# Turning all rows of the attention matrix on VectorE, and the identity in the diagonal tiles of adj, in a two-layer graph kernel

## The chip, the cores and the metric

The kernel runs on one core of one Trainium2 chip. The metric is the device time of one execution in microseconds. The kernel before was timed in three runs: median 2083.7 us, from 2083.01 to 2084.57. One more execution was profiled.

## What is computed

There are 3327 nodes with 256 features each and a weighted adjacency matrix adj. The first layer mixes over two graphs, in two steps, and the second is a graph attention layer with four heads. Cut to what matters:

```python
# layer 0, on h = relu(layernorm(x)); R = (adj + I) with rows scaled to sum 1
for n in range(2):
    logits = (Xa @ W1.T @ W2.T) @ (Xa @ W3.T).T
    probs = softmax(logits)
    A = probs kept down to the smallest set with sum >= 0.9, rows scaled to sum 1
    Xf = R @ Xf
    Xa = A @ Xa
    Z = Z + Xf @ U1[n].T + Xa @ U2[n].T
x = x + layernorm(h + Z) * ln_g + ln_b
# layer 1, on h = relu(layernorm(x)); hp = h @ W in 4 heads of 64; s, d from hp and a
e = leaky_relu(s[:, None] + d[None, :], 0.2), -inf where adj <= 0
x = x + elu(softmax(e) @ hp)
```

## The kernel before

The nodes are padded to 26 tiles of 128 (NT = 26, NP = 3328). Everything is f32. The fast path (function fast) is one list of pieces of work; a second, general path runs only if a check on the numbers at the end asks for it, and it doesn't here.

**Order.** Class Plan (L472) holds the pieces. put (L481) adds one with its engine, a planned length, a rank, the pieces it needs, the buffers it takes and gives, and a delay until others see its result (LAG). order (L507) plays this through in planned time, on each engine always taking the ready piece of lowest rank, and issue (L581) writes the instructions in the order found. The order on each engine's queue is therefore fixed when the program is built, and rests on the planned lengths. Pieces that issue nothing (a function `lambda: None`) join several needs or give back a buffer; they sit on SyncE's or GpSimd's list with lengths of 0.0 or 0.02. either (L500) leaves a piece to whichever of two engines is free.

**Stages.** First, x is loaded, normalised and projected (prepare, project_u). Then come two steps over the 26 rows of tiles (a row is 128 nodes against all 3328). Last, layer 1 runs in four blocks of 832 target nodes (attend_neighbours, L1629).

**A row of a step** (class Row, L873; search and attention, L1506 and L1563):
- TensorE makes the logits (L907) and ScalarE their exponentials in e, with sums (exps, L916). The pieces are 1024, 1024, 1024 and 255 wide.
- ScalarE counts entries above a guess, in passes over the whole row (L961, about 3 us each), GpSimd steps the guess on single columns, and VectorE collects the largest candidates (window, sort) and finds the threshold (choose, L1046). drop (L1074) sets what is under it to zero, in four pieces.
- e has then to be turned, since it stands with its targets on the partitions and TensorE needs its sources there. For rows under BLOCKED (all 26 of step one, 23 of step two), the first 24 tiles go through VectorE, in pairs of tiles interleaved element by element: turn_blocks (L1112) turns 32x32 blocks in place, put_blocks writes 1024 columns to blocks in DRAM, and get_blocks reads them back in four transfers, each onto 32 partitions. The last two tiles, and all 26 tiles of the other three rows, are turned by TensorE into a px bank (turn, L1084) and copied to et by ScalarE or VectorE (turned, L1097).
- attend_blocks (L1125) and attend (L1102) multiply with rhs into the bank acca.

**A full row** (class Full, L1139; full, L1604) is adj's row times Xf. adj comes in from HBM in seven loads of four tiles (load, L1146, four at buffers), and 26 products go to the bank accf (some, L1151). adj lacks the identity, so in step one add (L1181) adds the row's own tile and 1.0 to the sum, and in step two own (L1355) adds the row's own tile to ys before ys is stored.

**Layer 1.** Per block and source tile, ScalarE makes a mask from adj (L1753, L1754), VectorE writes masked exponentials for four heads in one e buffer (L1765), and TensorE multiplies: product (L1774) into the banks pl, sums (L1789) into acca and accf, sums after every second tile. After 26 tiles leave (L1839) copies the banks out, and seven pieces of 128 nodes are turned (L1868), divided, put through elu, added and stored.

Buffers on chip: e has four, used by rows and then by layer 1 (mine, L1814), which adds three more (e2) in the memory of c and rhs once the rows are done; px has two banks, et three buffers, at four.

Of the kernel before, what the change touches and what calls it, by code (L numbers as in the profile page):

```python
# [25 lines left out]
H = 4  # L26
# [23 lines left out]
BLOCKED = (NT, NT - 3)  # L50
# [421 lines left out]
class Plan:  # L472
# [3 lines left out]
    LAG = {"PE": 0.2, "ACT": 0.2, "DVE": 0.15, "POOL": 0.1, "SP": 2.2}  # L476
# [23 lines left out]
    def either(self, first, second, rank, *args, **kw):  # L500

        p = self.put(*first[:2], rank, first[2], *args, **kw)
        p["on"] = {e: (length, fn, self.LAG[e], 0.0) for e, length, fn in (first, second)}
        p["engine"] = ""
        return p
# [82 lines left out]
def fast(  # L588
# [58 lines left out]
    with ExitStack() as l0:  # L647
# [24 lines left out]
        blocks = spill.tile([3, 4, P, 2 * P], F32, name="blocks")  # L672
# [28 lines left out]
        def weights():  # L701
# [39 lines left out]
            a = plan.put("PE", 0.25, -200.0, turn, take=["px"], needs=[plan.put("SP", 0.02, -201.0, lambda: None, lag=8.0)])  # L741
# [126 lines left out]
        plan = Plan(dict(rows=1, mvs=3, pl=2, px=2, acca=1, accf=1, et=3, at=4, y=1, e2=3, mask=2, e5=1, qg=2, **BUFS))  # L868
# [4 lines left out]
        class Row:  # L873
# [3 lines left out]
                "b w t0 t1 t2 u g k2 p0 p1 p2 p3 D0 D1 D2 v z r0 s0 s1 s2 h x th tq mid dh kh fl d up h0 h1 room zs cnt "  # L877
# [38 lines left out]
            def exps(self, k):  # L916
                pl = self.pl.pop(k)
                to = self.e[:, PART * k : PART * k + pl.shape[1]]
                if k < 3 and self.i < BLOCKED[self.n]:
                    to = to.rearrange("p (g q t) -> p g t q", g=4, t=2)  # L920
                    pl = pl.rearrange("p (g t q) -> p g t q", g=4, t=2)
                S.activation(  # L922
                    to,
                    pl,
                    AF.Exp,
                    accum_out=(self.p0, self.p1, self.p2, self.p3)[k],
                )

            def row_sum(self):
                k = self.NAMES.index("p0")  # L930
                S.activation(self.sc[:, k + 4 : k + 8], self.sc[:, k : k + 4], AF.Copy, accum_out=self.s)
# [114 lines left out]
            def choose(self):  # L1046
# [14 lines left out]
                V.scalar_tensor_tensor(out_, win, nxt, keep, ALU.is_gt, ALU.mult, accum_out=self.cnt)  # L1061
                V.tensor_sub(self.m, met[:, 2, i], self.cnt)
                ties = small.tile([P, PIECES * 8], F32, name="rest", bufs=1).rearrange("p (c r) -> p c r", r=8)
                V.tensor_scalar(ties, self.cands, nxt, None, ALU.is_equal)
                num, upto = (small.tile([P, 4], F32, name=name, bufs=1) for name in ("num", "upto"))
                V.tensor_reduce(num[:, :3], ties[:, :15, :].rearrange("p (a c) r -> p a (c r)", a=3), AX.X, ALU.add)
                V.tensor_reduce(num[:, 3:], ties[:, 15, :], AX.X, ALU.add)
                V.tensor_tensor_scan(upto, num, num, 0.0, ALU.add, ALU.bypass)
                V.scalar_tensor_tensor(num, upto, self.m, num, ALU.is_le, ALU.mult, accum_out=met[:, 4, i])
                self.thr = small.tile([P, 4], F32, name="thr")  # L1070
                V.tensor_scalar(upto, upto, self.m, 2.0**-24, ALU.is_gt, ALU.mult)
                V.tensor_scalar(self.thr, upto, 1.0 - 2.0**-24, nxt, ALU.add, ALU.mult)

            def drop(self, o):  # L1074

                piece = self.e[:, o * PART : min((o + 1) * PART, N)]
                V.scalar_tensor_tensor(piece, piece, self.thr[:, o : o + 1], piece, ALU.is_gt, ALU.mult)  # L1077
# [6 lines left out]
            def turn(self, g):  # L1084
                m = min(4, NT - 4 * g)
# [1034 lines left out]
```

## Time and profile before

| | us |
|---|---|
| median of three runs | 2083.7 |
| the profiled execution, whole | 2085.48 |
| its span, first to last instruction | 2083.6 |
| TensorE busy in it | 2036.4 |
| VectorE busy | 1730.6 |
| ScalarE busy | 1298.7 |
| GpSimd busy | 999.0 |
| mean granted TensorE clock | 0.994 of full |

By time, the load and projection take about the first 90 us, the two steps run to about 1600 us, and layer 1 runs from about 1605 to the end. A line of a group in the prediction reads: line of the kernel, engine, operation, what is written and read with its shape, number, then busy time and mean ns of one, then the engine's idle time just before the group and what ended it. In a line of waits, the time in total is followed by the number of waits and the longest. In a line of stretches come the stretch and its length; busy time and number of instructions for TensorE's matmuls, its weight loads, VectorE, ScalarE and GpSimd; the granted clock; the DMA engines' busy share; and GB/s. An f32 matmul shows as two instructions, a transpose as one.

### The profile page before, as it was taken

Reading aid. Unit: us, or ns where it says so; the run is one execution under the profiler, and the core shown is the slowest. Engines: PE = TensorE matmul, PEld = TensorE weight load, DVE = VectorE, ACT = ScalarE, POOL = GpSimd, SP = SyncE. Lnnn points to the kernel's source line nnn. Section 1 sums busy time; section 2 is a strip of 40 time slices with the busy share of each in tenths; the row PEclk is TensorE's granted clock in tenths of the full one; section 3 lists DMA queues with packets and bytes.
Section 4 is the critical chain, followed back from the end, with each engine's and each line's share of the span. In section 5 each row is a group of like instructions: output and inputs, shape, how many; then the busy total and the mean of one; then the engine's idle time right before and its main releaser. Section 6 shows DMA issues by size and latency. Waiting matters only on the chain. (4 is left out here: it accounts for less than half of the span.)

```text
span 2083.6 us, 34334 instructions
## 1 busy us (share of the span) xinstructions
PE 2036.4 (98%) x10695; PEld 1417.9 (68%) x10695; DVE 1730.6 (83%) x4105; ACT 1298.7 (62%) x2480; POOL 999.0 (48%) x2170
## 2 busy tenths in 40 slices
PE   8999999999999999989999999999999999999997
PEld 6477778877787878767778787788877333333332
DVE  5689897778876871578998989988987999999895
ACT  5776665666556611777778776778662547474552
POOL 5476665456544620567878778787872000000001
PEclk9999999999999999999999999999999999999999
DMA  4166676557666674786666767677633444444341
GB/s 116 42 191 187 192 192 192 167 154 200 192 183 180 181 200 128 203 218 176 178 189 176 210 179 193 190 202 193 184 114 113 144 140 140 132 139 117 113 126 34
DMA packets 580513, 338.56 MB, mean 162 GB/s; under 512 B 327931, under 2 KB 533281, under 8 KB 580321
## 3 DMA queue, kind: packets, MB, share of 16 engines
q1 hardware_dynamic: 579424, 336.06, 57.3%
q8 instruction: 87, 1.43, 0.3%
q14 instruction: 106, 0.86, 0.2%
q10 hardware_dynamic: 896, 0.21, 0.0%
HBM read 242.86 MB, written 93.05 MB: 161 GB/s over the span
## 5 line engine op out<-in xcount | busy, mean ns | idle before, releaser
L961 ACT ACTIVATE junk<-e,sc 128x3327 fp8e5<-128x3327 f32 x147 | 450.9, 3067 | 26.2 <-POOL sc L998 24.7
L1130 PE MATMUL acca<-rhs,e 128*128 128x256 f32 x1872 | 426.9, 381 | 0.6 <-DMA e<-blocks 0.3
L1130 PEld LDWEIGHTS acca<-rhs,e 128*128 128x128 f32 x1872 | 365.7, 197 | 43.0 <-issue 3.5
L1155 PE MATMUL accf<-c,at 128*128 128x256 f32 x1352 | 315.0, 384 | 13.7 <-ACT main L1166 5.4
L1155 PE MATMUL accf<-main,at 128*128 128x257 f32 x1352 | 315.8, 383 | 3.0 <-ACT main L1306 2.5
L1155 PEld LDWEIGHTS accf<-c,at 128*128 128x128 f32 x1352 | 252.5, 191 | 63.0 <-ACT main L1166 8.4
L1155 PEld LDWEIGHTS accf<-main,at 128*128 128x128 f32 x1352 | 252.4, 191 | 51.9 <-issue 11.2
L1024 DVE MAX8 cands<-y 128x8 f32<-128x205 f32 (+1 forms) x832 | 243.1, 362 | 3.6
L1920 POOL TENSOR_TENSOR qq<-qq 128x256 f32<-128x256 f32 x4 | 3.0, 756 | 457.0 <-ACT qq L1916 457.0
L1019 DVE SCALAR_TENSOR_TENSOR y<-e,sc 128x1639 f32<-128x1639 f32 x84 | 165.1, 1965 | 57.4 <-POOL sc L1009 56.2
L922 ACT ACTIVATE e<-pl 128x1024 f32<-128x1024 f32 (+1 forms) x168 | 152.7, 919 | 77.6 <-PE pl L907 67.9
L1754 ACT ACTIVATE et<-at 128x448 bf16<-128x448 f32 (+1 forms) x204 | 112.5, 551 | 130.0 <-DVE e L1765 74.2
L1781 PE MATMUL pl<-e,main 128*64 128x416 f32 x1024 | 190.4, 517 | 0.1
L1077 DVE SCALAR_TENSOR_TENSOR e<-e,thr 128x1024 f32<-128x1024 f32 (+1 forms) x168 | 177.6, 1061 | 2.6 <-DMA qg<-kqs 0.2
L907 PE MATMUL pl<-kt,qg 64*128 64x512 f32 (+1 forms) x832 | 173.8, 536 | 0.3 <-ACT qq L922 0.3
L1114 DVE STREAM_TRANSPOSE e<-e 128x1024 f32<-128x1024 f32 x117 | 146.0, 1248 | 3.7
L1781 PEld LDWEIGHTS pl<-e,main 128*64 128x64 f32 x1024 | 70.3, 137 | 111.1 <-issue 92.3
L1765 DVE SCALAR_TENSOR_TENSOR e<-c,low,et 128x832 f32<-128x832 f32 x128 | 128.9, 1076 | 6.0 <-issue 3.2
L907 PEld LDWEIGHTS pl<-kt,qg 64*128 64x128 f32 x832 | 71.5, 186 | 83.2 <-issue 76.8
L1753 ACT ACTIVATE at<-at 128x448 f32<-128x448 f32 (+1 forms) x204 | 110.8, 543 | 24.7 <-DMA at<-in_adjt_dram 24.5
L1765 DVE SCALAR_TENSOR_TENSOR e<-qq,low,et 128x832 f32<-128x832 f32 x120 | 120.6, 1081 | 4.1 <-PE accf L1795 2.9
L961 ACT ACTIVATE junk<-qq,sc 128x3327 fp8e5<-128x3327 f32 x35 | 107.3, 3066 | 8.5 <-POOL sc L998 8.2
(550 smaller groups left out, 3550.5 us busy)
## 6 DMA issues: line engine op xcount, KB each, us to landing
at<-in_adjt_dram SPq DMA_DIRECT2D x414, 256.0 KB
blocks<-e SPq DMA_DIRECT2D x117, 512.0 KB
e<-blocks SPq DMA_DIRECT2D x468, 128.0 KB
at<-in_adjt_dram SPq DMA_DIRECT2D x102, 192.0 KB
blocks<-qq SPq DMA_DIRECT2D x30, 512.0 KB
qq<-blocks SPq DMA_DIRECT2D x120, 128.0 KB
at<-in_adjt_dram SPq DMA_DIRECT2D x52, 128.0 KB
ys<-ystage SPq DMA_DIRECT2D x26, 256.0 KB
```

What stands on the lines that cost most here:

```text
L907: T.matmul(pl[:, lo : lo + m], qg[self.n, self.i // 4][half, self.i % 4, :], kt[half, 512 * k : 512 * k + m], start=True, stop=True,)
L922: S.activation(to, pl, AF.Exp, accum_out=(self.p0, self.p1, self.p2, self.p3)[k],)
L961: S.activation(junk[:, :N], self.e[:, :N], fn, bias=t, scale=-1.0, accum_out=dst, saturate=False)
L1019: V.scalar_tensor_tensor(self.y[:, : hi - lo], self.e[:, lo:hi], self.up, self.e[:, lo:hi], ALU.is_lt, ALU.mult, accum_out=(self.h0, self. ...
L1024: V.max(self.cands[:, a * PIECES // 2 + k, :], self.y[:, at[k] - lo : at[k + 1] - lo])
L1077: V.scalar_tensor_tensor(piece, piece, self.thr[:, o : o + 1], piece, ALU.is_gt, ALU.mult)
L1114: V.transpose(part, part)
L1130: T.matmul(self.acc, lhs, rhs[self.n][:, j, :], start=(j == 0), stop=stop and j == js[-1])
L1155: T.matmul(self.acc[:, : self.w], self.at[j // JC][:, j % JC, :], self.src[:, j, : self.w], start=(j == 0), stop=(j == NT - 1),)
L1754: S.activation(to, src, AF.Sign)
L1765: V.scalar_tensor_tensor(held["e"][:, k, :], extra["both"][b % 2][:, k, :], low[:, j, k : k + 1], held["mask"], ALU.max, ALU.mult,)
L1781: T.matmul(q["acc"][a][k * FH : (k + 1) * FH, c, :C], main[:, j, h * FH : (h + 1) * FH], held["e"][:, h, c * C : (c + 1) * C], start=(j == 0),
```

## The change

All rows are turned through VectorE and DRAM, and turn, turned and attend are gone. A row now has three parts of 1024, 1024 and 1280 columns, for dropping, turning and the round trip. The last piece of exponentials is written in two halves to the interleaved places, so there are five partial sums for four. choose finds the threshold of each piece by a running count over all 128 candidates, in fewer instructions, and failures checks accordingly.

GpSimd adds the identity to the diagonal tile of each row of adj after it is loaded (diagonal). The additions of the own tile are gone from take, add and finish1. In finish2, ScalarE scales by qd straight from the bank, in four parts, and VectorE's scale is gone.

In the plan, pieces that issue nothing have their own list "" with length 0, many lengths and delays are set anew, and full rows of step one get later ranks. In layer 1 one of the extra buffers (ec, in the memory of c) may be used before all rows are done, the first two source tiles are ranked before the last rows of step two, and the sums of block 0 wait for all rows. In the last block the last six tiles (LATE) are done for the first 416 nodes and then for the other 416, and each half is copied out by itself.

The diff, cut to its core:

```diff
-    LAG = {"PE": 0.2, "ACT": 0.2, "DVE": 0.15, "POOL": 0.1, "SP": 2.2}
+    LAG = {"PE": 0.2, "ACT": 0.2, "DVE": 0.15, "POOL": 0.1, "SP": 2.2, "": 0.0}
...
-        plan = Plan(dict(rows=1, mvs=3, pl=2, px=2, acca=1, accf=1, et=3, at=4, y=1, e2=3, mask=2, e5=1, qg=2, **BUFS))
+        plan = Plan(dict(rows=1, mvs=3, pl=2, px=2, acca=1, accf=1, et=3, at=4, y=1, e2=2, ec=1, mask=2, e5=1, qg=2, **BUFS))
...
+                if k < 3:
+                    S.activation(to, pl.rearrange("p (g t q) -> p g t q", g=4, t=2), AF.Exp, accum_out=sums[k])
+                else:
+                    S.activation(to[:, 0, 0, :], pl[:, :P], AF.Exp, accum_out=self.p3)
+                    S.activation(to[:, 0, 1, : m - P], pl[:, P:], AF.Exp, accum_out=self.p4)
...
-                V.scalar_tensor_tensor(out_, win, nxt, keep, ALU.is_gt, ALU.mult, accum_out=self.cnt)
-                V.tensor_sub(self.m, met[:, 2, i], self.cnt)
-                ties = small.tile([P, PIECES * 8], F32, name="rest", bufs=1).rearrange("p (c r) -> p c r", r=8)
-                V.tensor_scalar(ties, self.cands, nxt, None, ALU.is_equal)
-                num, upto = (small.tile([P, 4], F32, name=name, bufs=1) for name in ("num", "upto"))
-                V.tensor_reduce(num[:, :3], ties[:, :15, :].rearrange("p (a c) r -> p a (c r)", a=3), AX.X, ALU.add)
-                V.tensor_reduce(num[:, 3:], ties[:, 15, :], AX.X, ALU.add)
-                V.tensor_tensor_scan(upto, num, num, 0.0, ALU.add, ALU.bypass)
-                V.scalar_tensor_tensor(num, upto, self.m, num, ALU.is_le, ALU.mult, accum_out=met[:, 4, i])
-                self.thr = small.tile([P, 4], F32, name="thr")
-                V.tensor_scalar(upto, upto, self.m, 2.0**-24, ALU.is_gt, ALU.mult)
-                V.tensor_scalar(self.thr, upto, 1.0 - 2.0**-24, nxt, ALU.add, ALU.mult)
+                V.scalar_tensor_tensor(out_, win, nxt, keep, ALU.is_equal, ALU.mult, accum_out=self.m)
+                ties = small.tile([P, PIECES * 8], F32, name="rest", bufs=1)
+                V.tensor_scalar(ties, self.cands.rearrange("p c r -> p (c r)"), nxt, None, ALU.is_equal)
+                V.tensor_tensor_scan(ties, ties, ties, 0.0, ALU.add, ALU.bypass)
+                self.thr = small.tile([P, PIECES], F32, name="thr")
+                V.tensor_scalar(self.thr, ties[:, 7::8], self.m, 2.0**-24, ALU.is_gt, ALU.mult)
+                V.tensor_scalar(self.thr, self.thr, 1.0 - 2.0**-24, nxt, ALU.add, ALU.mult)
+                ends = ties[:, 39:80:40]
+                V.scalar_tensor_tensor(ends, ends, self.m, ends, ALU.is_equal, ALU.mult, accum_out=met[:, 4, i])
...
+            def diagonal(self):
+                own = self.at[self.t // JC][:, self.t % JC, :]
+                GP.tensor_add(own, own, ident)
...
             def take(self):
                 self.f = small.tile([P, H * FH + 2 * H], F32, name="f", bufs=BUFS["f"])
-                V.tensor_add(self.f[:, :D], self.acc[:, :D], self.src[:, self.t, :D])
-                V.tensor_copy(self.f[:, D : D + 1], self.acc[:, D:])
-                self.added = True
+                V.tensor_copy(self.f[:, : self.w], self.acc[:, : self.w])
...
-            a = plan.put("DVE", 0.43, r + 0.3, own, needs=[a, fulls[t]], hold=0.4)
-            y = plan.put("SP", 0.5, r + 0.3, store, needs=[a], give=["ystage"], lag=3.0)
+            y = plan.put("SP", 0.5, r + 0.3, store, needs=[a], give=["ystage"], lag=7.0)
...
-                f = held["f"] = small.tile([P, H * FH + 2 * H], F32, name="f", bufs=BUFS["f"])
-                S.copy(f, held["pm"])
-                S.activation(qd[:, t, :], f[:, H * FH + H :], AF.Exp)
-                S.activation(low[:, t, :], f[:, H * FH + H :], AF.Exp, scale=ALPHA - 1.0)
+                pm = held["pm"]
+                S.activation(qd[:, t, :], pm[:, H * FH + H :], AF.Exp)
+                for k in range(H):
+                    part = slice(k * FH, (k + 1) * FH)
+                    S.activation(main[:, t, part], pm[:, part], AF.Copy, scale=qd[:, t, k : k + 1])
+                S.activation(low[:, t, :], pm[:, H * FH + H :], AF.Exp, scale=ALPHA - 1.0)
+                S.copy(sd[:, :, t, :], pm[:, H * FH :].rearrange("p (k h) -> p k h", k=2))
...
+            come = []
+            for g in range(3):
+                b = plan.put(
+                    "DVE", 1.17 if g < 2 else 1.44, rank - 1.001, row.turn_blocks, g, needs=[drops[g]]
                 )
+                b = plan.put("SP", 0.5, rank - 1.0, row.put_blocks, g, needs=[b], lag=8.0)
+                b = plan.put("", 0.0, -90.0, lambda: None, needs=[b], lag=0.0)
+                come.append(
+                    [plan.put("SP", 0.6, rank - 1.0, row.get_blocks, g, o, needs=[b], lag=5.5) for o in range(4)]
+                )
+            for j in range(0, NT - 2, 4):
+                js = range(j, j + 4 if j < 20 else NT)
                 a = plan.put(
+                    "PE", 0.432 * len(js), rank, row.attend_blocks, js, needs=[come[j // 8], a, right],
+                    take=["acca"] * (j == 0), give=[own_e[row.n][row.i]] * (j == 20),
                 )
...
+            a, own = None, plan.put("POOL", 0.4, -90.0, f.diagonal, needs=[loads[t // JC]])
             for j in range(0, NT, 2):
                 last = j % JC == JC - 2 or j == NT - 2
                 a = plan.put(
-                    "PE", 0.437 * 2, rank, f.some, range(j, j + 2), needs=[a, loads[j // JC], right[j : j + 2]],
+                    "PE", 0.437 * 2, rank, f.some, range(j, j + 2), needs=[a, loads[j // JC], right[j : j + 2], own if t in (j, j + 1) else None],
                     take=["accf"] * (j == 0), give=["at"] * last,
                 )
...
+                    if b == 3 and j >= NT - LATE:
+                        for c in range(2):
+                            r = rank if c == 0 else r0 + 9.0
+                            p_ = plan.put("PE", 0.71, r, product, 0, (c,), needs=[x_, last_acc, halves[c]])
+                            p_ = plan.put("PE", 0.71, r, product, 1, (c,), needs=[x_, y_, p_])
+                            halves[c] = plan.put(
+                                "PE", 0.76, r, sums, (c,), needs=[p_, last_den], give=[mine] if c else []
+                            )
+                        continue
...
-                full(n, t, (min(1.0 + 1.15 * t, 27.0) if n == 0 else base + 1.0 + t), [p[0] for p in sources], [p[1] for p in sources] if n == 0 else loaded[0])
+                full(n, t, (2.0 + 1.3 * t if n == 0 else base + 1.0 + t), [p[0] for p in sources], [p[1] for p in sources] if n == 0 else loaded[0])
```

## The prediction, made before the changed kernel ran

> **What bounds the kernel now.** I read the page's first part, then TensorE's groups with their shapes apart, then what TensorE waited for, then stretches of the span, then the timeline around the longest waits and the end.
>
> ```profile
> span 2083.6 us, 34334 instructions
> PE 2036.4 (98%) x10695; PEld 1417.9 (68%) x10695; DVE 1730.6 (83%) x4105; ACT 1298.7 (62%) x2480; POOL 999.0 (48%) x2170
> ```
>
> TensorE is busy 98% of the span, but its matmul ends are modelled, so I checked it by the distance from one start to the next in the trace's records. It is 216 ns (median; least 215) for each half of an f32 matmul of 256 columns, whether its left side came through TensorE (L1107) or through blocks (L1130), and 109 ns for a transpose; a record lasts 381 and 273 ns because neighbours overlap. TensorE therefore runs back to back, and the time is its work plus its gaps. The groups that the change touches, and a neighbour:
>
> ```profile
> L1130 PE MATMUL acca<-rhs,e 128*128 128x256 f32 x1872 | 426.9, 381 | 0.6 <-DMA e<-blocks 0.3 <-issue 0.2
> L1107 PE MATMUL acca<-rhs,et 128*128 128x256 f32 x352 | 86.2, 380 | 0.3 <-ACT xa L1134 0.3
> L1089 PE MATMUL px<-ident,e 128*128 128x128 f32 x156 | 27.5, 285 | 5.2 <-ACT ystage L1349 5.0 <-DVE e L1077 0.3
> L1089 PE MATMUL px<-ident,qq 128*128 128x128 f32 x20 | 4.0, 280 | 0.2 <-DVE qq L1077 0.2
> ```
>
> The 156 + 20 at L1089 are the transposes of e. The gaps, by TensorE's waits:
>
> ```profile
> PE accf L1155 <- ACT main L1166: 5.4, 5, 3.4
> PE px L1089 <- ACT ystage L1349: 5.0, 1, 5.0
> PE accf L1155 <- DMA at<-in_adjt_dram: 5.0, 1, 5.0
> PE accf L1155 <- DVE main L1169: 3.3, 3, 1.4
> ...
> PE accf L1155 <- ACT main L1306: 2.5, 1, 2.5
> ```
>
> All gaps over 0.1 us sum to 36.9 us: 7 to 8 in the first 45 us, 1.2 at the end, about 28 from 90 to 1550 us. Four of these are long (2.5 at 92 us, 5.0 at 736, 5.0 at 892, 3.35 at 1545, sum 15.8), and the clock answers them. The stretches around them, against undisturbed ones:
>
> ```profile
> 736.00:747.10 11.10, 6.13 (x17) 4.74 (x16) 7.43 (x21) 3.65 (x3) 5.83 (x10) 0.69 0.41 135
> 891.90:900.70 8.80, 3.83 (x11) 3.00 (x11) 8.59 (x21) 5.85 (x6) 7.03 (x15) 0.81 1.00 237
> 1544.50:1552.70 8.20, 4.85 (x19) 3.63 (x18) 7.69 (x27) 4.15 (x6) 5.83 (x12) 0.79 0.77 262
> 98.60:736.00 637.40, 636.95 (x2958) 505.32 (x2956) 536.96 (x1451) 414.24 (x750) 370.02 (x799) 1.00 0.67 186
> 1604.60:2068.90 464.30, 464.20 (x3393) 169.49 (x3392) 429.73 (x488) 251.19 (x597) 5.54 (x6) 1.00 0.43 125
> ```
>
> The clock is 0.69 to 0.81 in the first three and 1.00 in the others. The trace's clock records put it at one half for 17 us in all after the four waits (3.4, 6.8, 3.4, 3.4), some 8 us of work lost. Waits and slow clock make these four places worth about 24 us.
>
> [...]
>
> **The change part by part, against the profiled span of 2083.6.**
> 1. *Transposes leave TensorE.* 49 rows x 2 and 3 rows x 26 = 176, x 109 ns = 19.2 us. All lie on the engine that is never free, so all of it comes off. The matmuls behind them keep their number and 216 ns. **-19.2.**
> 2. *VectorE.* Transposes: 147 x 1.248 = 183 now, 52 x (2 + 1.25) x 1.248 = 211 after, +28. Drops: per row 3 x 1.265 + 0.45 = 4.24 becomes 3.25 x 1.265 = 4.11, -7. choose: the instructions from L1061 to L1072 take 1.93 us from start to start; in their place come a product with sum (0.33), a scan of 128, two small scalings (0.24 each) and one with sum (0.32). The scan is not in the trace: 24 elements take 207 ns and 32 take 273, by which 128 would take from 0.3 (4 elements: 178, so nearly flat) to 1.07 (that slope); I take 0.4, so 1.53 and -21 over 52 rows (+15 to -26). Copies of transposes (12.6), the self term at L1185, L1174 and L1186 (12.0), L1357 (12.6) and the scaling at L1457 and L1458 (15.7) go. Sum about -52 of 1731. VectorE is not what TensorE waits for (its releases in the list come to 5 us), so directly 0; it is slack against new waits.
> 3. *ScalarE, GpSimd, DMA.* ScalarE loses 18.9 us of copies at L1100 and gains about 0.3 x 52 for the split exponentials and 0.6 x 26 for scaling, +12 of 1299. GpSimd gains 52 additions of the identity; between 287 ns (128x1) and 826 ns (128x256) I take 0.55, 29 us on an engine that is busy 48%. DMA: the round trip goes from 49 x 12 to 52 x 13 tiles, 150 to 173 MB or 8% of the traffic in those stages, whose DMA share is 0.66. All beside TensorE: 0. If GpSimd's cover is gone, see rival 4.
> 4. *Waits that change.* The 5.0 us at 736 is a transpose of e that wants a px bank; the bank is held because ScalarE's copy to ystage waits for the store of ys (33 us of such waits at L1349). The transpose is gone, and the store no longer waits for the self term; that wait goes. The other three are results that stand behind a 3.06 us count on ScalarE (L1306, L1166) or a load that came late: matters of order. The order is planned anew: durations in it now meet the trace (transposes 1.17 for 1.25 planned, copies of exponentials 1.07), the store's delay is 7 for 3, and empty steps no longer take turns on SyncE and GpSimd. Bounds: all four places go (-24) or as many new ones come (+20 and more); I take half, **-12**.
> 5. *End of step two.* The last three rows now take the round trip. From the end of VectorE's transpose to the first matmul that uses it is 13.7 us at best and 18 in the median now, where TensorE's own path began within 2 us of the drops. The last row would be ready some 10 us later. Cover: products of stage three that need no sums. The five e buffers (four e, one ec) allow 5 x 2.8 = 14 us, with the first two tiles' masks ranked early. Bounds 0 and +12; **+3.**
> 6. *Last block of stage three.* The period of two tiles is 8.67 us, of which 8.38 is 64 half matmuls and 0.29 two changes of shape. Six tiles in 12 halves have 24 changes for 6, 18 x 0.145 = +2.6. After the last sum 4 of 7 pieces remain; these are spaced 0.75 us, so 3 x 0.75 = -2.3. Bounds -4 and +3; **0.**
>
> Sum -19.2 - 12 + 3 = -28, span 2055.4. The profiled run took 2085.5, the median is 2083.7; taking the difference from the median gives **2055**.
>
> **Rivals.**
> 1. *Most gaps go.* For it: one wait's cause is removed, and the plan's figures are nearer the trace. Against: a fixed order on six queues always misses somewhere. 2083.7 - 19.2 - 24 - 4 = 2036.
> 2. *The gain is half given back.* New waits of about 20 us take the place of the old (late blocks, a bank, ScalarE's counts). [...] 2083.7 - 19.2 + 10 = 2074.
> 3. *TensorE's transposes were free.* If they sat in gaps, nothing but the waits moves: about 2083. Against: 109 ns from start to start, with neighbours following directly.
> 4. *Slower: the identity.* Each full product now waits at tile t for a GpSimd addition. GpSimd works in order and stands up to 6.5 us before counts (91.5 us in 28 waits at L991). Pairing the loads of at with the first matmul that reads each, in order, 63 of 364 are used less than 6 us after issue, the median 13.0. If the addition came 1 us late in each of 52 products, +52 - 28: 2108. It decides from 28/52 = 0.54 us on average. Against: the order takes it ahead of other GpSimd work, and most loads have 8 us to spare.
>
> **How the numbers follow.** Forecast 0.54 (own range 2044 to 2067), rival 1 0.19, rival 2 0.15, rival 3 0.03, rival 4 0.09. Up to 2079 and down to 2034 leaves out rivals 3 and 4 and the lower part of rival 1, 2 in 10. What a measurement can tell is 0.2%, or 4 us. Faster than 2079.5: 0.86; slower than 2087.9: 0.10; between: 0.04.
>
> **What would show it.** Step 1: no transposes of e, 10519 TensorE instructions, still 216 ns apart. Step 2: VectorE near 1680 us busy. Step 4: fewer than four stretches of half clock, and no wait of px for ystage. Step 5: gaps around 1550 to 1610 us, released by blocks or e. Step 6: under 15 us from the last sum to the end. Rival 4: waits of accf for GpSimd on at. It is wrong if TensorE's gaps sum to over 65 us, whatever releases them, or if a 256-column half matmul is spaced otherwise than 216 ns.

## The result and the profile after

| | before | changed | ratio, 95% interval |
|---|---|---|---|
| median, first comparison | 2084.1 us (4 runs) | 2071.4 us (4 runs, 2066.6 to 2077.0) | 0.9944 [0.992, 0.9969] |
| the changed kernel again, another chip (e1) | 2081.7 us | 2072.5 us (6 runs) | 0.9952 [0.9938, 0.9967] |

The forecast was 2055. The change gains 9 to 13 us where 28 were forecast. The direction held, and so did the outer range of 2034 to 2079; the forecast's own range of 2044 to 2067 did not, nor did the size. The first part of the page, after:

```profile
span 2075.2 us, 33982 instructions
...
PE 2025.6 (98%) x10519; PEld 1401.3 (68%) x10519; DVE 1696.3 (82%) x3768; ACT 1298.7 (63%) x2630; POOL 1040.1 (50%) x2222
```

TensorE has the 10519 instructions that were forecast, 176 fewer, and is busy for the same 98% of a span that is only 8.4 us shorter. Its groups with shapes apart:

```profile
L1100 PE MATMUL acca<-rhs,e 128*128 128x256 f32 x2184 | 485.6, 380 | 4.1 <-DMA e<-blocks 2.3 <-DVE y L1016 1.1 <-ACT main L1139 0.6
L1125 PE MATMUL accf<-main,at 128*128 128x257 f32 x1352 | 323.8, 389 | 14.1 <-DMA at<-in_adjt_dram 7.6 <-POOL at L1132 3.3 <-ACT f L1136 1.7
L1125 PE MATMUL accf<-c,at 128*128 128x256 f32 x1352 | 308.6, 382 | 5.9 <-DMA at<-in_adjt_dram 2.2 <-POOL at L1132 2.2 <-ACT main L1139 1.1
```

The groups of transposes are gone, a record of L1100 (attend_blocks) lasts 380 ns, and starts still lie 216 ns apart. So the saved work is what was forecast. What moved stands behind the bars. L1125 is the product of a full row, L1155 in the kernel before; the lines with main are step one's, those with c step two's:

```profile
L1155 PE MATMUL accf<-main,at 128*128 128x257 f32 x1352 | 315.8, 383 | 3.0 <-ACT main L1306 2.5 <-ACT f L1162 0.5
L1155 PE MATMUL accf<-c,at 128*128 128x256 f32 x1352 | 315.0, 384 | 13.7 <-ACT main L1166 5.4 <-DMA at<-in_adjt_dram 5.0 <-DVE main L1169 3.3
```

Step one's products stand idle for 14.1 us where it was 3.0, mostly for loads of adj and for the identity, and step two's for 5.9 where it was 13.7. TensorE's waits of the changed kernel, longest first (us in total, times, longest):

```profile
PE accf L1125 <- DMA at<-in_adjt_dram: 9.8, 7, 4.2
PE accf L1125 <- POOL at L1132: 5.5, 3, 2.7
PE acca L1732 <- ACT xa L1104: 4.5, 1, 4.5
PE pl L906 <- ACT e L921: 2.4, 2, 1.3
PE acca L1100 <- DMA e<-blocks: 2.3, 2, 1.4
```

The 5.0 us for ystage and the waits for counts (main) that headed the list before are gone or small. In their place stand loads of adj, the identity's addition (L1132) and one copy of the last row's result (L1104). All gaps over 0.1 us sum to 40.2 us, for 36.9 before. The stretches around the longest, and an undisturbed one (columns as in the prediction):

```profile
753.00:758.00 5.00, 4.89 (x15) 4.09 (x16) 0.00 (x0) 0.00 (x0) 0.00 (x0) 0.66 1.01 246
783.00:793.50 10.50, 7.96 (x23) 5.22 (x24) 1.92 (x6) 1.84 (x4) 0.89 (x1) 0.67 0.63 210
1519.00:1525.00 6.00, 4.41 (x13) 3.33 (x14) 5.89 (x11) 0.60 (x1) 5.41 (x9) 0.72 1.07 252
1592.00:1604.00 12.00, 7.46 (x48) 2.68 (x48) 6.69 (x9) 5.81 (x12) 2.23 (x2) 0.86 0.68 217
98.60:736.00 637.40, 632.65 (x2900) 499.80 (x2899) 546.22 (x1375) 420.15 (x783) 409.48 (x845) 1.00 0.72 198
```

The clock is 0.66 to 0.86 in the first four. Stretches of half clock ahead of the tail sum to 23.9 us in six places, for 17.1 in four. In the first and third the DMA engines' busy share is 1.01 and 1.07.

**Stalls, the measure used below.** For each TensorE instruction I took the distance from its start to the next one's, less the undisturbed distance of that shape (216 ns for 256 columns, 109 ns for a transpose, 443 ns at a change of the tile's shape). The sum holds gaps and lost clock together. It is 71.9 us before and 82.5 after. So the span's -8.4 is -19.0 of work and +10.6 of stalls. Work here is counted, not measured: it is what the instructions would take at the undisturbed distances. Stalls by stretch of each kernel's own span, with those of the experiments:

| profiled execution | 0-110 | 110-680 | 680-960 | 960-1480 | 1480-1620 | to the end | sum |
|---|---|---|---|---|---|---|---|
| before | 15.9 | 4.3 | 21.3 | 13.9 | 8.9 | 7.5 | 71.9 |
| before, figure of PE 0.21 (e13) | 13.2 | 4.1 | 20.5 | 11.8 | 8.3 | 7.4 | 65.4 |
| before, figure of ACT 0.21 (e14) | 13.4 | 3.8 | 12.2 | 14.0 | 8.1 | 7.4 | 59.0 |
| changed | 18.9 | 7.5 | 21.7 | 8.9 | 16.8 | 8.7 | 82.5 |
| changed, figure of PE 0.21 (e12) | 17.2 | 7.5 | 19.5 | 11.6 | 23.6 | 8.7 | 88.1 |
| changed, figure of ACT 0.21 (e15) | 18.7 | 7.5 | 19.6 | 8.1 | 23.2 | 8.7 | 85.7 |
| changed, old ranks (e8) | 16.5 | 5.0 | 11.9 | 20.3 | 30.5 | 8.7 | 92.9 |
| last row by TensorE (e10) | 16.7 | 6.6 | 19.3 | 7.3 | 10.2 | 8.4 | 68.5 |
| last three rows by TensorE (e6) | 16.4 | 6.5 | 16.2 | 8.6 | 4.0 | 8.3 | 60.0 |
| the same, ranks between (e11) | 17.4 | 8.2 | 11.3 | 13.5 | 7.0 | 8.6 | 66.0 |
| the same, figure of PE 0.21 (e16) | 17.8 | 8.2 | 12.5 | 18.5 | 4.4 | 8.6 | 69.9 |

Each sum belongs to one profiled execution. The changed kernel's was the slowest of its four (2077.0 us, median 2071.4) and e6's the fastest of its five (2063.8 us, median 2069.1), so a sum can lie some us off what is usual for its kernel. Of one stretch less depends on this: worked out the same way, other profiles of the changed kernel's order up to there (e1, e3 and e7) give 14 to 17 us from 1480 to 1620, for its 16.8.

### The profile page after: what moved, and what is told of

Same layout as the page of the kernel before. It is cut to its first block, busy times and chain, and to the rows that moved or that the text cites. A ratio compares the mean times of both kernels' runs of the same rounds, so it can differ in the third digit from the quotient of the medians.

```text
span 2075.2 us, 33982 instructions
## 1 busy us (share of the span) xinstructions
PE 2025.6 (98%) x10519; PEld 1401.3 (68%) x10519; DVE 1696.3 (82%) x3768; ACT 1298.7 (63%) x2630; POOL 1040.1 (50%) x2222
## 5 line engine op out<-in xcount | busy, mean ns | idle before, releaser
L1100 PE MATMUL acca<-rhs,e 128*128 128x256 f32 x2184 | 485.6, 380 | 4.1 <-DMA e<-blocks 2.3
L1100 PEld LDWEIGHTS acca<-rhs,e 128*128 128x128 f32 x2184 | 427.9, 197 | 49.4 <-issue 3.5
L1125 PE MATMUL accf<-main,at 128*128 128x257 f32 x1352 | 323.8, 389 | 14.1 <-DMA at<-in_adjt_dram 7.6
L1125 PE MATMUL accf<-c,at 128*128 128x256 f32 x1352 | 308.6, 382 | 5.9 <-DMA at<-in_adjt_dram 2.2
L1125 PEld LDWEIGHTS accf<-main,at 128*128 128x128 f32 x1352 | 253.4, 193 | 76.6 <-issue 19.0
L1125 PEld LDWEIGHTS accf<-c,at 128*128 128x128 f32 x1352 | 252.4, 190 | 57.1 <-issue 8.9
L1016 DVE SCALAR_TENSOR_TENSOR y<-e,sc 128x1639 f32<-128x1639 f32 x84 | 167.5, 1994 | 65.4 <-POOL sc L1006 64.4
L1718 PE MATMUL pl<-e,main 128*64 128x416 f32 x1024 | 191.6, 517 | 0.0
L921 ACT ACTIVATE e<-pl 128x1024 f32<-128x1024 f32 x126 | 137.8, 1101 | 64.5 <-PE pl L906 54.7
L1084 DVE STREAM_TRANSPOSE e<-e 128x1024 f32<-128x1024 f32 (+1 forms) x126 | 168.7, 1339 | 7.1 <-DVE e L1072 0.5
L1072 DVE SCALAR_TENSOR_TENSOR e<-e,thr 128x1024 f32<-128x1024 f32 (+1 forms) x126 | 170.7, 1354 | 1.5 <-issue 0.4
L1718 PEld LDWEIGHTS pl<-e,main 128*64 128x64 f32 x1024 | 69.3, 137 | 109.8 <-issue 93.7
L1690 ACT ACTIVATE at<-at 128x448 f32<-128x448 f32 (+1 forms) x204 | 110.6, 542 | 45.5 <-DMA at<-in_adjt_dram 45.4
L1104 ACT ACTIVATE xa<-acca,sc 128x256 f32<-128x256 f32 x52 | 24.3, 467 | 151.3 <-PE acca L1100 151.2
```

The costliest lines, as they stand in the source:

```text
L921: S.activation(to, pl.rearrange("p (g t q) -> p g t q", g=4, t=2), AF.Exp, accum_out=sums[k])
L1016: V.scalar_tensor_tensor(self.y[:, : hi - lo], self.e[:, lo:hi], self.up, self.e[:, lo:hi], ALU.is_lt, ALU.mult, accum_out=(self.h0, self. ...
L1072: V.scalar_tensor_tensor(piece, piece, self.thr[:, at : at + 1], piece, ALU.is_gt, ALU.mult)
L1084: V.transpose(part, part)
L1100: T.matmul(self.acc, lhs, rhs[self.n][:, j, :], start=(j == 0), stop=(j == NT - 1))
L1125: T.matmul(self.acc[:, : self.w], self.at[j // JC][:, j % JC, :], self.src[:, j, : self.w], start=(j == 0), stop=(j == NT - 1),)
```

## The experiments

Each was timed against the kernel before on its own chip; ratios are to that. All start from the changed kernel unless it says otherwise.

### Are the new waits a few with causes of their own? (e1 to e4)

Theory A: the waits that came are few, each from a part of the change, and go with it. Theory B: they belong to the fixed order as a whole, and where one is taken away the next takes over. e1 is the changed kernel as it is. 

> The changed kernel once more, unaltered, as the measure for the others. Both theories: 2071 us, between 2066 and 2077. If the spread comes from the half-clock stretches, each execution's span is lower the higher its mean clock, about 10 us between 0.992 and 0.998.

e2 keeps the order and leaves the identity out of 50 of the 52 full rows, so that their sums lack it:

```diff
-                GP.tensor_add(own, own, ident)
+                if self.t == NT - 1:
+                    GP.tensor_add(own, own, ident)
```

> The order of every queue is that of the changed kernel; the identity is left out of the diagonal tiles of adj in 50 of 52 full rows (only the last tile's rows keep it). Theory A, the shortfall is a few waits of their own: the GpSimd waits of 5.5 us and the half clock after two of them go, 2071 becomes 2062 to 2066. Theory B, TensorE's waits belong to the order as a whole and the next one (loads of at, a bank) takes over: 2069 to 2072.

e3 was to issue the last row's copy out of acca ahead of layer 1's masks on ScalarE. In the changed kernel TensorE ended that row at 1593.2 us. What followed is seen in two timelines of the changed kernel (start, length, engine, line, operation, tiles, count, the idle time before it and what ended it). TensorE's:

```profile
1593.12 1.62 PE L1718 MATMUL pl<-e,main 128*64 128x416 f32 x8
1599.27 1.30 PE L1732 MATMUL acca<-e,qd 128*32 128x416 f32 x8 [4.54 <-ACT xa L1104]
```

and ScalarE's:

```profile
1596.70 0.63 ACT L1690 ACTIVATE at<-at 128x512 f32<-128x512 f32 x1 [4.79 <-DMA at<-in_adjt_dram]
...
1598.76 0.46 ACT L1104 ACTIVATE xa<-acca,sc 128x256 f32<-128x256 f32 x1
```

The copy that frees the bank is an instruction of 0.46 us, but it stands in ScalarE's queue behind a mask (L1690) whose adj arrived at 1596.7.

```diff
+        k = max(k for k, p in enumerate(order) if p["fn"].__name__ == "attended")
+        to = max(j for j, p in enumerate(order[:k]) if p in order[k]["needs"]) + 1
+        order.insert(to, order.pop(k))
```

> One instruction is moved: the copy that takes the last row's sums out of acca stands on ScalarE directly behind the piece that it waits for, ahead of the masks of layer 1 that stood in its way. Theory A: the wait of 4.5 us at 1599 us goes with the half clock behind it, some 6 us, 2071 becomes 2065. Theory B: the masks that now come later hold VectorE's exponentials and TensorE stands for them instead, 2069 to 2072.

This edit changed no queue. It moves the copy forward in the list of pieces, but only past pieces of other engines: the masks ahead of it on ScalarE stand ahead of the row's last product in that list too. In e3's trace every engine issues the same instructions in the same order as in the changed kernel, and the copy (L1108 there) still follows the mask (L1694 there):

```profile
1592.71 0.63 ACT L1694 ACTIVATE at<-at 128x512 f32<-128x512 f32 x1 [3.32 <-DMA at<-in_adjt_dram]
...
1594.77 0.46 ACT L1108 ACTIVATE xa<-acca,sc 128x256 f32<-128x256 f32 x1
```

So e3 is the changed kernel once more, and what the copy's place costs was not tested.

e4 is e2 and e3 together (identity left out as in e2), and so in effect e2 once more. 

> Both edits (identity left out of 50 of 52 full rows, and the copy out of acca moved ahead). Theory A: the two gains add, 2057 to 2061. Theory B: 2067 to 2071.

| | median us | ratio | stalls us |
|---|---|---|---|
| e1 | 2072.5 | 0.9952 [0.9938, 0.9967] | 80.2 |
| e2 | 2070.8 | 0.9947 [0.9934, 0.9961] | 76.6 |
| e3 | 2072.6 | 0.9948 [0.9929, 0.9967] | 78.6 |
| e4 | 2073.1 | 0.9954 [0.9936, 0.9972] | 80.1 |

None is told apart from e1. With one order on TensorE, the single waits differ from one execution to the next: TensorE waits for the last row's copy 4.5 us in the changed kernel's first profile, 5.0 in e1, 2.3 in e3, 4.5 in e2 and 3.6 in e4, and for adj 9.8, 11.9, 11.6, 12.3 and 15.3 us. TensorE's waits in e4 (L1104 is L1108 there):

```profile
PE accf L1129 <- DMA at<-in_adjt_dram: 15.3, 10, 4.1
...
PE acca L1737 <- ACT xa L1108: 3.6, 1, 3.6
```

For the identity, theory A falls: it asked for 2062 to 2066 in e2. The additions take 30.1 us of GpSimd (52 x 579 ns), and leaving out 50 of them saves nothing that can be measured. For the copy, neither theory was tested. That other waits grew because these went, as theory B has it, is not shown either, since waits differ by some 3 us between executions of one order.

### Were the transposes worth 19 us? (e5)

The kernel before, each transpose of e done twice:

```diff
-                    T.transpose(pt[:, k, :], self.e[:, j * P : (j + 1) * P], ident)
+                    for _ in range(2):
+                        T.transpose(pt[:, k, :], self.e[:, j * P : (j + 1) * P], ident)
```

> The kernel before, in its own order, with each of its 176 TensorE transposes of e done twice. Theory P (the transposes lie on the path in full; the change took 19.2 us away and waits gave some back): 176 x 109 ns = +19 us, 2099 to 2103, and TensorE's gaps within 3 us of before. Theory F (the transposes stood in gaps, so that taking them away was worth much less than 19.2): under +8 us, below 2091.

It took 2098.6 us for 2082.2, ratio 1.0076 [1.0063, 1.009], that is +13 to +19 us. The time is just under theory P's 2099 and far above theory F's 2091: the transposes lie on the path, nearly in full. In the profiled executions the span grew by 13.8, and the stalls fell by 4.8 (P had the gaps within 3 us). So the transposes that the change removed were worth about their 19 us, and what was lost of the forecast was lost in waits.

### Where do the waits come from? (e6 to e12)

e6 turns the last three rows of step two by TensorE again, as before. 

> The changed kernel with the last three rows of step two turned by TensorE again, as before (78 transposes, +8.5 us of work; the rest of the order planned anew). Theory C (the round trip of these rows costs what the stretch 1480 to 1620 lost, 16.8 us against 8.9): the stretch returns to 9, so +8.5 - 8 = no change, 2069 to 2074. Theory B (waits belong to the order as a whole; those of the last rows are not the round trip's own): the stretch keeps 14 or more and the work is added, 2077 to 2081.

e7 sets the last block as before:

```diff
-            LATE = 6
+            LATE = 0
```

> The changed kernel with the last block as before (LATE = 0). The forecast's sum for this part was +2.6 - 2.3 = 0: without it the stretch before the last sums is 2.6 us shorter and the end 2.3 to 3 us longer, 2069 to 2074. If the halves cost nothing in the block, 2074 to 2077; if they are dearer than they bring, 2066 to 2069.

e8 gives step one's full rows their old ranks:

```diff
-(2.0 + 1.3 * t if n == 0 else base + 1.0 + t)
+(min(1.0 + 1.15 * t, 27.0) if n == 0 else base + 1.0 + t)
```

> The changed kernel with the ranks of step one's full rows as before. Theory D (the later ranks are what makes TensorE wait for adj's loads at 750 to 790 us: full rows run back to back there while the load queue is filled with blocks and layer 1's arrays): the two waits of 2.7 and 4.2 us and one stretch of half clock go, 2060 to 2066. Theory B (order as a whole): other waits take over, 2068 to 2076.

| | median us | ratio |
|---|---|---|
| e6, last three rows by TensorE | 2069.1 | 0.9938 [0.9925, 0.9951] |
| e7, last block as before | 2069.9 | 0.9943 [0.993, 0.9956] |
| e8, old ranks | 2090.4 | 1.0046 [1.0033, 1.0058] |

e6 does 8.5 us more work on TensorE and takes no more time: the stalls at 1480 to 1620 us fall from 16.8 to 4.0. That is theory C. The plan was drawn anew with these rows, and the stretch 680 to 960 fell too (21.7 to 16.2), so not all of e6's time need be theirs. The stretch 1480 to 1620 us, in the columns of the stretches above, the last three being clock, DMA share and GB/s. Of the kernel before:

```profile
1480.00:1620.00 140.00, 134.68 (x686) 107.58 (x688) 113.75 (x295) 68.22 (x116) 75.14 (x152) 0.99 0.48 139
```

Of the changed kernel:

```profile
1480.00:1620.00 140.00, 129.26 (x648) 95.44 (x649) 120.15 (x242) 66.62 (x126) 70.68 (x131) 0.98 0.76 217
```

Of e6:

```profile
1480.00:1620.00 140.00, 137.86 (x767) 99.27 (x767) 111.66 (x243) 67.32 (x141) 55.61 (x116) 1.00 0.46 135
```

Over the whole span the round trips of three more rows are a small part of the traffic (10.2 of 361.6 MB, by the estimate below). In this stretch they stand beside layer 1's first loads and take the DMA share from 0.48 to 0.76, and TensorE is busy 129.3 us for 134.7. The rise fits in size: from 139 to 217 GB/s over 140 us is 10.9 MB, and three rows of 26 tiles of 64 KB, written and read back, are by estimate 10.2 MB.

e8 is the clearest lesson. The waits at 750 to 790 us did shrink (680 to 960: 21.7 to 11.9 us), as theory D said, and the kernel became 18 us slower, far outside both theories' times. TensorE's timeline near the end of step two:

```profile
1545.90 8.51 PE L1125 MATMUL accf<-c,at 128*128 128x256 f32 x38
1556.30 0.92 PE L1125 MATMUL accf<-c,at 128*128 128x256 f32 x2 [1.89 <-POOL at L1132]
1567.73 3.75 PE L1100 MATMUL acca<-rhs,e 128*128 128x256 f32 x8 [10.51 <-DMA e<-blocks]
...
1575.32 7.93 PE L1100 MATMUL acca<-rhs,e 128*128 128x256 f32 x36
1583.18 1.62 PE L1718 MATMUL pl<-e,main 128*64 128x416 f32 x8
1591.83 7.75 PE L1718 MATMUL pl<-e,main 128*64 128x416 f32 x24 [7.03 <-DVE e L1702]
```

The last full row (L1125) ends at 1557.2; two rows of L1100 are still to come, the first of them waits 10.5 us for its blocks, and there is nothing else to do. Layer 1's products (L1718), which the prediction took as cover, wait 7.0 us themselves for exponentials that VectorE makes after the last row's drops. In this order full rows' products were the stock of work that could have covered a late round trip; used up early, they were missing at the end.

e9 is e6 and e8 together. 

> The changed kernel with the last three rows turned by TensorE and the ranks of step one's full rows as before, e6 and e8 together. Theory G (full rows' products are a stock of work that can stand in for a late row; with the old ranks it is used up before the last rows, so e8 stood still at the end; rows turned by TensorE need no such stock): the end keeps e6's stall of about 4 us and the step's boundary e8's 12 in place of 16 to 22, 2056 to 2066. Theory B (whatever is mended, other waits of the order take over): e6's time or worse, 2068 to 2080.

e10 turns only the last row by TensorE. 

> The changed kernel with only the last row of step two turned by TensorE (26 transposes, +2.8 us). Theory C1 (only the last row's round trip lies open, as earlier rows have other rows behind them): the stretch 1480 to 1620 falls to 4 to 7 us of stalls, 2062 to 2068. Theory C3 (the three rows stand back to back and each of them is open): the stretch keeps 10 or more, 2070 to 2076.

e11 has the last three rows by TensorE and ranks between:

```diff
-(2.0 + 1.3 * t if n == 0 else base + 1.0 + t)
+(1.5 + 1.22 * t if n == 0 else base + 1.0 + t)
```

> The last three rows turned by TensorE and ranks of step one's full rows between old and new (1.5 + 1.22 t). Theory G: between e6 and e9, stalls moving smoothly from the end to the boundary of the steps. Theory B: off that line by 4 us or more to either side.

e12 moves one figure of the plan:

```diff
-    LAG = {"PE": 0.2, "ACT": 0.2, "DVE": 0.15, "POOL": 0.1, "SP": 2.2, "": 0.0}
+    LAG = {"PE": 0.21, "ACT": 0.2, "DVE": 0.15, "POOL": 0.1, "SP": 2.2, "": 0.0}
```

> The changed kernel with one figure of the plan moved a little (TensorE's results are seen 0.21 us later for 0.20), which gives another order with the same work. Theory B: another set of waits, its sum off by 3 to 8 us to either side, so a time in 2064 to 2080 that differs from the changed kernel's 2072 by more than 2. Theory A (the waits are few and each has a cause of its own that this doesn't touch): within 2 us of 2072, with the same longest waits at the same places.

| | median us | ratio |
|---|---|---|
| e9, e6 and e8 together | 2077.7 | 0.9973 [0.9964, 0.9983] |
| e10, last row by TensorE | 2070.2 | 0.9942 [0.9929, 0.9956] |
| e11, last three rows, ranks between | 2068.6 | 0.9937 [0.9923, 0.9951] |
| e12, one figure of the plan | 2080.5 | 0.999 [0.9982, 0.9998] |

e9 keeps both mendings in place (10.7 us at 680 to 960, 9.4 at 1480 to 1620) and pays 22.9 between them, where e6 paid 8.6. Theory G's time fails: other waits stand in between, and what they have in common was not followed up. In e10 the last row alone takes 6.6 us of stalls away for 2.8 of work, and in e6 three rows take 12.8 for 8.5. Stretch (10.2) and time lie at C3's lower edge: the last row has the largest part, but not the whole. e11 has the lowest median of all, but its interval overlaps that of the changed kernel. From 680 on, its stalls lie between e6's and e9's in each of the three stretches, as theory G said (11.3, 13.5 and 7.0); its time does not, it is e6's within the noise.

e12 takes back 8 us of the changed kernel's gain with the same work, as theory B said. TensorE's waits in it:

```profile
PE accf L1125 <- DMA at<-in_adjt_dram: 20.7, 7, 9.0
```

and its timeline at the longest of them:

```profile
1545.53 1.13 PE L1125 MATMUL accf<-c,at 128*128 128x256 f32 x4 [1.31 <-POOL at L1132]
1555.69 5.38 PE L1125 MATMUL accf<-c,at 128*128 128x256 f32 x12 [9.03 <-DMA at<-in_adjt_dram]
```

### Was the order before a lucky one? (e13 to e16)

If the order before was a lucky draw for its work, any new plan would bring waits. So the same small moves were made in the kernel before (e13: PE 0.21, e14: ACT 0.21), in the changed one (e15: ACT 0.21) and in e11 (e16: PE 0.21), each by one figure as in e12.

> The kernel before with the plan's figure for TensorE's results at 0.21 for 0.20, nothing else. Theory S (the order before was one of the lucky ones for its work, so that planning anew, whatever the change, brings waits back): slower than before by 5 to 15 us, 2087 to 2097. Theory N (orders of this work lie around before by chance): within 5 us to either side, 2077 to 2087.

> The kernel before with the plan's figure for ScalarE's results at 0.21 for 0.20. Theory S: 2087 to 2097. Theory N: 2077 to 2087.

> The changed kernel with the plan's figure for ScalarE's results at 0.21 for 0.20. With e12 (2080.5) it gives the spread of the changed work over orders. If its order was lucky too: 2077 to 2087; if orders lie around it by chance: 2066 to 2077.

> e11 (last three rows turned by TensorE, ranks between) with the plan's figure for TensorE's results at 0.21 for 0.20. Theory G (taking the round trip out of the last rows takes away the open end whatever the order): the stretch 1480 to 1620 keeps 10 us of stalls or less, 2064 to 2073. Theory B (a draw like any other): as e12 against the changed kernel, 2074 to 2082.

| | median us | ratio |
|---|---|---|
| e13, before, PE 0.21 | 2079.1 | 0.9988 [0.9981, 0.9994] |
| e14, before, ACT 0.21 | 2074.8 | 0.9966 [0.9953, 0.9979] |
| e15, changed, ACT 0.21 | 2079.3 | 0.9988 [0.9981, 0.9995] |
| e16, e11 with PE 0.21 | 2072.0 | 0.9952 [0.9939, 0.9965] |

Theory S falls: both new orders of the kernel before are faster than it. It is the changed kernel whose order was the best of its three. Three orders of each: before 2082.1, 2079.1 and 2074.8, mean 2078.7; changed 2072.5, 2080.5 and 2079.3, mean 2077.4. The means are 1.3 us apart, and orders of one kernel up to 8, so three orders each can't tell the change's gain over all orders from nothing. In their profiles the stalls grew by 20 us in the mean (65.4 to 85.4); the changed kernel's profiled executions were by chance some 3 us slower than its medians, so 17 is nearer, almost what the transposes had cost. Most of that is one stretch, 1480 to 1620: 8.1 to 8.9 us in the three orders of before, 16.8 to 23.6 in these three of the changed kernel, 4.0 to 7.0 in e6, e11 and e16. The same stretch of e14, an order of the kernel before, shows the DMA share that goes with it, 0.45 again:

```profile
1480.00:1620.00 140.00, 135.41 (x725) 102.29 (x726) 115.25 (x266) 69.72 (x119) 64.46 (x124) 0.99 0.45 131
```

e16 keeps 4.4 us there and takes 2072.0 us with the figure that gave e12 2080.5. So turning the last three rows on TensorE mended the end in each of the three orders tried with the new ranks or those between. These three, 2068.6 to 2072.0 us, are also faster than the kernel before in any of its orders; with the old ranks (e9) it is not so.

### Is the late load of adj a matter of SyncE's queue? (e17, e18)

SyncE's timeline in e12, around the 9.0 us that TensorE waited for a load of adj:

```profile
1539.97 2.07 SPq L1667 DMA_DIRECT2D kt<-in_adjt_dram  x4
1542.09 1.14 SPq L1634 DMA_DIRECT2D qq<-highs  x2
...
1543.84 2.66 SPq L1119 DMA_DIRECT2D at<-in_adjt_dram  x2
1546.55 7.44 SPq L1093 DMA_DIRECT2D e<-blocks  x4
1554.09 2.07 SPq L1119 DMA_DIRECT2D at<-in_adjt_dram  x1
```

The trace's semaphores tell which load it was. TensorE went on when the first of the two loads issued at 1543.84 had landed, at 1555.6. It was 11.7 us on its way; the median of such loads in e12 is 3.7, with which it would have come 0.9 us into the wait. It stands ahead of the four reads of blocks (L1093), not behind them as the expectation of e17 has it. Ahead of it are layer 1's transfers: of these the two broadcasts (L1634, 832 KB each) took 8.5 and 9.9 us to land. e17 is e12 with layer 1's transfers (L1634 and L1667, 12 in the traces where the expectations count 20) on ScalarE's queue and the same order of TensorE, VectorE and GpSimd; e18 does it to e11.

```diff
-                        nc.sync.dma_start(
+                        nc.scalar.dma_start(
                             extra["both"][b % 2][:, 2 * a : 2 * a + 2, :],
...
-                            nc.sync.dma_start(
+                            nc.scalar.dma_start(
                                 extra["at"][:, j, t0 * P : (t1 - 1) * P + w].rearrange("p (i q) -> p i q", q=w),
```

> e12, with the same order on TensorE, VectorE and GpSimd, but layer 1's broadcast loads and first columns of adj (20 transfers) issued by ScalarE instead of SyncE. e12 waits 9.0 us at 1546 us for a load of adj; that load stands on SyncE behind four reads of blocks, and these behind six transfers for layer 1 issued from 1540 us on. Theory Q (what stands ahead in SyncE's queue is the cause): the wait falls under 4 us, 2073 to 2077. Theory W (the DMA engines' bandwidth is the cause, wherever a transfer is issued): the wait stays at 7 us or more, 2078 to 2083.

> e11 with the same 20 transfers issued by ScalarE. Theory Q: shorter stalls behind loads of adj and blocks near the end, 2064 to 2068. Theory W: within 2 us of e11's 2068.6; if ScalarE's own work is held up by the issues, 2070 to 2075.

e17 took 2071.0 us, 0.9946 [0.9933, 0.9959]; e18 2073.6, 0.9955 [0.9943, 0.9967]. e17's wait is still there, in TensorE's timeline:

```profile
1549.78 4.35 PE L1125 MATMUL accf<-c,at 128*128 128x256 f32 x12 [8.08 <-DMA at<-in_adjt_dram]
```

and SyncE's of e17:

```profile
1535.83 2.09 SPq L1119 DMA_DIRECT2D at<-in_adjt_dram  x2
1539.51 7.68 SPq L1093 DMA_DIRECT2D e<-blocks  x4
1547.28 2.90 SPq L1119 DMA_DIRECT2D at<-in_adjt_dram  x1
```

The load awaited is again the first of the pair ahead of the reads. Issued at 1535.83, it landed 13.8 us later, though layer 1's transfers had left its queue, and the DMA share from 1535 to 1556 us is 0.92, for 0.81 in e12. So for this wait theory Q falls: what took the time was the transfer under way, not its place in SyncE's queue. Bandwidth, theory W, fits. In e12, what was issued from the first broadcast to the last of the four reads is 3.4 MB, which by estimate takes 12 us at the 280 GB/s moved from 1539 to 1556. That the broadcasts are the part that matters, and that issuing them later would help, was not tried.

Yet e17 is 9.5 us faster than e12, which W did not expect. In the spans (10.8 us) 5.0 had come before that wait, 0.9 came at it, and 4.9 after it, where a wait of 2.4 us for L1104 and its slow clock are gone. Why the stretch before the wait, with the same order of the compute engines, became shorter is open. e18 is 5 us slower than e11, so the move is no general gain; its time lies where the expectation put a hold-up of ScalarE's own work, which was not followed up.

## Why the prediction was right in direction and wrong in size

1. *Transposes, -19.2.* Right: the instructions went as forecast and stayed 216 ns apart, and in e5 the same number the other way costs 13 to 19 us of time.
2. *VectorE, about -52, worth 0.* Its parts came near their prices: choose -18 for -21, the 32x32 transposes +25 for +28, the scan 0.45 us for 0.4. The busy time on the page fell by only 34, in part since groups that the sum left out grew. TensorE's waits for VectorE come to 5 us as before, so little of the loss is VectorE's.
3. *ScalarE, GpSimd, DMA, 0.* ScalarE stayed level for +12 and GpSimd grew by 41 for 29, of which the identity is 30.1. The traffic grew from 338.6 to 361.6 MB, the +23 forecast (the round trip itself is 154 and 177 MB, where the prediction has 150 and 173). "All beside TensorE: 0" holds for the identity (e2) and not for the traffic: a share over the whole steps hid that 1480 to 1620 went from 0.48 to 0.76.
4. *Waits, -12.* This is the step that failed. I counted the four long waits of one execution as something that a new plan would halve. The ystage wait did go, as forecast, and the one at the first full row stayed (98 us), but four new ones came, at 753, 785, 1519 and 1599 us. Stretches of half clock ahead of the tail are six for four, where fewer than four were to be the sign. Outside the end of step two, the stalls rose by 2.7 us where -12 was forecast. e13 and e14 show what new orders of the old work give: stalls of 65.4 and 59.0 for 71.9, a gain of 3 to 7 us, without the change. A plan drawn anew moved the time by up to 8 us either way, which is most of the term.
5. *End of step two, +3.* The second failure, in the cover. Bounds were 0 and +12; the stretch 1480 to 1620 grew by 7.9 us, and by about 15 in the other two orders. The longest waits there are not for blocks, as forecast, but for adj's loads at 1519 us and for the copy behind a late mask at 1599: the round trips met layer 1's loads (DMA share 0.76 for 0.48). The cover named, layer 1's products, came to wait for VectorE itself in e8 (7.0 us).
6. *LATE, 0.* Right: e7, without it, is within 3 us of the changed kernel. The end after the last sum went from 14.7 to 11.7 us, and 15.6 in e7.

So in the profiled pair the -8.4 us are step 1's -19, less +7.9 at the end of step two and +2.7 of other waits: more before 680 us (+6.2), fewer from 960 to 1480 (-5.0). What brought those before 680 us is open beyond their names in the list. That the gain came out at 13 and not lower is in part luck of the draw: the same work in the orders of e12 and e15 gains 2 and 3 us. Rival 2, "the gain is half given back", at 2074 with new waits named as late blocks and counts, is nearest to what came; late loads of adj were the largest single item. Rival 4 didn't come: three waits for the identity sum to 5.5 us, a mean of 0.1 us over 52 products for the 0.54 from which it decides. The bound that was to show the forecast wrong, gaps over 65 us, was too wide to show it: gaps of 40 were enough.

## What to carry to other kernels

When a kernel's order is fixed by a plan, work taken off the bounding engine and waits brought by a new order are two results: draw a few orders of both versions by a tiny move of one figure before reading a gain of half a per cent as the change's own. A transfer that is free in the middle of a stage can be dear at its end (with the new round trips the stalls fell by 5.0 us at 960 to 1480 us, and rose by 7.9 at 1480 to 1620); read the DMA share and the other work at hand in that stretch, and follow the work you name as cover to what it waits for itself. When an edit is to change an order, look in the trace whether any queue changed: e3's did not. And where a load is late, ask first which load it was and when it was issued. Doing the last rows the dearer way, with less latency, can be worth its work (in e6 8.5 us of work, for 12.8 us fewer stalls at 1480 to 1620).

## What the hardware showed that was not expected

Executions of one program spread with the clock. In the first comparison the changed kernel's spans ran from 2064.8 us at a mean clock of 0.998 to 2075.2 at 0.992; in e1 from 2068.0 at 0.995 to 2075.2 at 0.992, but not in strict order (2070.2 at 0.993, 2073.4 at 0.994), so e1's expectation holds only roughly. The clock records of the changed kernel's first profile have five stretches of half clock at waits of 2 to 5 us: 3.41 us at waits of 2.73 us (ending at 97.9 us), 2.66 (753.1), 2.15 (1519.5) and 4.54 (1599.3), and 6.83 us at one of 4.17 (785.5). No wait over 2 us is without one there. It was not always so: the wait at the first full row was followed by one in the changed kernel's first profile (2.73 us), and not in e1's (2.4 us). Ahead of the sixth stretch, 3.41 us at 12.5 us, the longest waits are 1.8 us at the start of the span and 1.02 us at 10.9. And ahead of the half clock at 1521 us TensorE had been busy for 0.7 of the 3.41 us before. Ahead of the tail the stretches of both kernels' profiles are all 3.41 or 6.83 us long. What decides whether a wait is followed by one was not shown.

A DMA issue on SyncE took 0.43 us in the median of the changed kernel's first profile, and 0.37 to 0.51 us in the middle half. In e12, where the DMA share was 0.81, the four reads of blocks took 0.8, 3.2, 2.0 and 1.3 us, and the load behind them in the queue was issued only at 1554.09 us, 7.5 us after the first of them. The same four reads in e17, at a share of 0.92, took 0.3 to 0.5 us each, and were spread over 7.7 us because SyncE waited in between, 4.6 us of it for a write of blocks to land.
